# Listing the far tokens earlier, all row statistics between search rounds, normalising before the scatter

## The chip, the cores and the metric

The kernel runs on one core of a Trainium2 chip. The metric is device time in microseconds (us) of one launch: the median of three runs. The engines are PE (matrix products), DVE (VectorE, elementwise work), ACT (ScalarE, functions and scaled copies), POOL (GpSimd, here scatters, gathers and some additions) and SP (SyncE, here transfers only). Each works through its own queue in order and waits on semaphores for the others.

## The reference

Four images of 64 x 64 positions ("tokens", 4096 an image) with 256 channels. A deformable convolution comes first, then additive attention over each image's tokens, then a feed-forward layer on the higher-weighted half of the tokens only:

```python
# layer 0: x = x + conv(gn(x)); inside conv, every position, group and tap reads
samples = _bilinear_sample(img, sg)          # at learned offsets
out = (samples * m).sum(-1)                  # mask from a softmax over 9 taps
...
# layer 1
t = t + _L1_attn_ref(_ln_t(t), Wt, Wx, bh, Wa, ba)
t = t + _L1_ffn_ref(_ln_t(t), mask, wr, br, w1, b1, w2, b2)
...
def _L1_ffn_ref(x, attention_mask, wr, br, w1, b1, w2, b2):
    weights = (jnp.einsum('bsd,do->bso', x, wr) + br)[..., 0]
    _, idx = jax.lax.top_k(weights, k)       # k = half of 4096
    sel_idx = idx[:, :kk]                    # kk = k - 1
    sel = jnp.take_along_axis(x, sel_idx[:, :, None], axis=1)
    h = jax.nn.gelu(jnp.einsum('bkd,dh->bkh', sel, w1) + b1)
    y = jnp.einsum('bkh,hd->bkd', h, w2) + b2
    y = y * jnp.take_along_axis(weights, sel_idx, axis=1)[..., None]
    return jnp.zeros_like(x).at[batch_idx, sel_idx].set(y) + x
```

## The kernel before, in words

A first stage computes offsets and interpolation weights for all images, a second the convolution of image 0 (`sample_image(0, 6)`). Then a loop over the images n = 0 to 3 has two scopes each. In the first, three generators are stepped in turn by a string of letters (`turns`, L1418):

- "m" is `feed_forward(n - 1)` (L1244). It loads the attention's result as `v2` in 8 transfers (32 tiles of 128 tokens), takes 32 dot products `pr`/`tdot` with the router's weights (L1257, four steps of 8), forms the weights `wa`, and searches for the 2047th largest in 8 rounds of 4 bits each (`kth_largest`, L1201; a step per round). A round compares all weights with 15 candidates on DVE, sums over partitions with PE (`pcn`) and picks a digit. Then it turns two masks into positions (`positions`, L516, two matmuls and a prefix sum of 12 short operations), ends with the row numbers `rif`, and POOL scatters 32 tiles into sorted order in DRAM (`sort_d`, L1300); all that is the step after the last round. The next step writes the normalised tokens of all rows as `base` (ACT, L1312) to the output. Then it takes the sorted rows in chunks of 512: SP loads a chunk (`big<-sort`, L1332), which waits for all 32 scatters, ACT normalises it (L1340), PE transposes and multiplies.
- "o" is `attention_prep(n)` (L783). One step loads the tokens `v`; eight steps do `row_stats` of 4 tiles each (bn_stats and bn_aggr on DVE); one step makes the reciprocal deviation `lnr` (ACT, then DVE) and the shift `lnm`, and has ACT normalise the 32 tiles in place (L802). Then come three steps for each of 8 units: `units` (16 transposes `ptt` on PE, a copy `vT` to SBUF on DVE, a product `pq`), `products` (`pk`, `pf` on PE, `kf`, `qe` on ACT, a transfer `qf<-qe`, a minimum `least` on DVE), and `below_zero` (`mm` on DVE).
- "s" is `sample_image(n + 1)` (L668), empty for n = 3. Its first step is `list_tokens` (L534): some tokens' offsets are too far for the regular interpolation, and are listed. Flags `fl` become slots `sl` by `positions`, and 32 one-hot comparisons `oh` (DVE), each with a matmul into `pl` (PE), gather the listed tokens' numbers; `ls` and `uf` follow. The later steps are interpolations: a multiplication with interpolation weights `wb` (L697, one transfer of 512 KB each from SP, two buffers) and an addition (L705); `exact_rows` (L566 on) computes the listed tokens exactly, beginning with some 25 small DVE operations and a gather `rw` on POOL.

Operations of "m" and "o" on DVE are pinned: they keep their program order among themselves (L259). Those of `list_tokens` and `exact_rows` are not; the scheduler places them on DVE from where they stand in the program. For n = 0 another string is used, and m is empty. In the second scope of each image, attention runs (over 2000 us), with the rest of the "s" steps beside it. At the end, the feed-forward of image 3 runs alone.

The places in question are the three transitions between attentions: T1 (n = 1, lists image 2), T2 (n = 2, lists image 3) and T3 (n = 3, lists none). The lists of images 0 and 1 run in the convolution stage of image 0.

Of the kernel before, what the change touches and what calls it, by code (L numbers as in the profile page):

```python
# [9 lines left out]
F32 = mybir.dt.float32  # L10
I32 = mybir.dt.int32
AF = mybir.ActivationFunctionType
ALU = mybir.AluOpType
# [3 lines left out]
P = 128  # L17
NB, H, W, C = 4, 64, 64, 256
L = H * W
NT = L // P  # L20
# [25 lines left out]
def layers_kernel(ctx: ExitStack, tc: tile.TileContext, a, out: bass.AP):  # L46
    nc = tc.nc
# [162 lines left out]
    tok = cb.tile([P, NT, 2], F32, name="tok")  # L210
    slotr = cb.tile([P, P], F32, name="slotr")
# [22 lines left out]
    S = SimpleNamespace(bank=True, wants=False, gather=True, left=0, tables=[])  # L234

    def bank_taken():
        S.wants = not S.bank
        return S.wants

    @contextmanager  # L240
    def scope(*pools):

        with ExitStack() as st:
            for name, bufs, psum in pools:
                kw = {"space": PSUM} if psum else {}
                setattr(S, name, st.enter_context(tc.tile_pool(name=name, bufs=bufs, **kw)))
            yield
            for name, _, _ in pools:
                delattr(S, name)
# [267 lines left out]
    def positions(fl, vec):  # L517

        pp = S.ps_m.tile([P, 2, NT], F32, tag="pm", name="pp")
        nc.tensor.matmul(pp[:, 0, :], below, fl, start=True, stop=True)  # L520
        nc.tensor.matmul(pp[:, 1, :], ones, fl, start=True, stop=True)
        before = [S.two.tile([P, NT], F32, tag=f"bf{i}", name=f"bf{i}") for i in range(2)]
        vec.tensor_copy(before[0], pp[:, 1, :])
        for i in range(5):
            w = 1 << i
            vec.tensor_copy(before[1][:, :w], before[0][:, :w])
            vec.tensor_add(before[1][:, w:], before[0][:, w:], before[0][:, : NT - w])
            before.reverse()
        sl = before[1]
        vec.tensor_sub(sl, before[0], pp[:, 1, :])  # L530
        vec.tensor_add(sl, sl, pp[:, 0, :])
        return sl, before[0][:, NT - 1 :]

    def list_tokens(n):  # L534

        while bank_taken():
            yield  # L540
        fl = S.two.tile([P, NT], F32, tag="fl", name="fl")
        nc.vector.tensor_scalar(fl, omax[:, n, :], 1.0, None, ALU.is_gt)
        sl, total = positions(fl, nc.vector)
        nc.vector.tensor_copy(large[:, n : n + 1], total)

        nc.vector.tensor_scalar(sl, sl, 1.0, None, ALU.add)
        nc.vector.tensor_mul(sl, sl, fl)
        nc.vector.tensor_scalar(sl, sl, -1.0, None, ALU.add)
        pl = S.ps_m.tile([P, 2], F32, tag="pm", name="pl")
        for i in range(NT):  # L550
            oh = S.sb.tile([P, P], F32, tag="oh", name="oh")
            nc.vector.tensor_scalar(oh, slotr, sl[:, i : i + 1], None, ALU.is_equal)
            nc.tensor.matmul(pl, oh, tok[:, i, :], start=(i == 0), stop=(i == NT - 1))
        ls = S.two.tile([P, 2], F32, tag="ls", name="ls")
        nc.vector.tensor_copy(ls, pl)

        uf = S.smp.tile([P, 1], F32, tag="uf", name="uf")
        nc.vector.tensor_mul(uf, ls[:, 1:2], spare)
        nc.vector.tensor_sub(uf, spare, uf)
        nc.vector.tensor_add(uf, uf, ls[:, 0:1])  # L560
        return uf
# [106 lines left out]
    def sample_image(n, depth=1):  # L668
# [3 lines left out]

        S.left = STEPS
        uf = yield from list_tokens(n)
        yield
        exact = []
# [63 lines left out]
    def sample_any(n):  # L740

        num = nc.values_load(large[0:1, n : n + 1], min_val=0, max_val=L)
        with tc.If(num > P), scope(
            ("smp", 2, 0), ("two", 2, 0), ("sb", 2, 0), ("dn", 1, 0), ("ps_t", 1, 1), ("ps_m", 1, 1)
        ):
            cur = S.two.tile([P, 1], F32, tag="cur", name="cur")
            nc.vector.tensor_copy(cur, part)
            with tc.For_i(0, NT, 1):
                exact = []
                for _ in exact_rows(n, cur, exact):  # L750
                    pass
                put_rows(n, *exact[0])
                nc.vector.tensor_scalar(cur, cur, float(P), None, ALU.add)
# [649 lines left out]
    for n in range(NB):  # L1403
        with scope(("att", 1, 0), ("smp", 2, 0), ("dn", 1, 0)):
            v = S.att.tile([P, NT, C + 1], F32, name="v")
            kf = S.att.tile([P, 2, L], F32, name="kf")

            sampling = sample_image(n + 1) if n + 1 < NB else iter(())
            S.gather = False
            with scope(  # L1410
                ("one", 1, 0), ("two", 2, 0), ("sb", 2, 0), ("row", 2, 0), ("rp", 3, 0),
                ("ps_d", 2, 1), ("ps_n", 1, 1), ("ps_m", 3, 1),
            ):


                main = feed_forward(n - 1, pinned) if n else iter(())
                prep = attention_prep(n, v, kf, pinned)
                if n:  # L1418
                    turns = (
                        "mo" + "m" * 5 + "mo" * 6 + "m" + "ooo" + "s" + "oss" * 2 + "m" + "oss" * 7 + "m" + "oss" * 3  # L1420
                        + ("m" + "ossss" * 3 + "msss" * 4) * 4
                    )
                else:
                    turns = "o" * 10 + "s" + "os" * 24
                for turn in turns:
                    next({"m": main, "o": prep, "s": sampling}[turn], None)
                for rest in (main, prep):
                    for _ in rest:
                        pass
            S.gather = True  # L1430
            with scope(
                ("two", 2, 0), ("sb", 2, 0), ("rp", 6, 0), ("qp", 2, 0),
                ("ep", 2 * PVB + 1, 0), ("ap", 1, 0), ("ps_d", 2, 1), ("ps_n", 3, 1), ("ps_m", 1, 1),
            ):
                attention(n, v, kf, [sampling])
        attention_any(n)
        if n + 1 < NB:
            sample_any(n + 1)
# [39 lines left out]
```

## Time and profile before

| | us |
|---|---|
| median of 3 runs | 10557.95 |
| lowest and highest | 10553.36, 10569.91 |
| the profiled execution | 10563.61 |
| its span | 10561.9 |

The first transition, in the same execution (the last column is T2, where it was read):

| event | T1 | T2 |
|---|---|---|
| first DVE operation of the transition | 3615.64 | 5918.98 |
| weights `wa` begin | 3631.30 | 5932.86 |
| `rif`, the last thing before the scatter | 3679.97 | 5981.53 |
| first scatter on POOL | 3680.43 | 5982.00 |
| last scatter ends | 3720.7 | 6022.3 |
| list's result `ls` | 3730.93 | 6033.36 |
| third `vT` of the preparation | 3751.25 | 6053.69 |
| first operation on chunk 0 (`si`) | 3773.59 | 6075.91 |
| attention begins on PE | 3978.79 | 6280.00 |

How to read a line of a timeline: start in us, busy time in us, engine, source line, operation, written tile <- read tiles, shapes, count, and in brackets the idle time before it with what ended it. "issue" there means that the engine waited for nothing that the profile shows; "remote" names no instruction either; "DMA" with tiles is a transfer. A line that begins with a stretch A:B has its length and then busy time (and count) of each engine, the granted TensorE clock, the DMA engines' share of busy time and GB/s.

### The profile page before, as it was taken

The page shows a single profiled execution, that of the slowest core. Times are in us where ns is not written, and L with a number is a line of the kernel's source. Part 1 is how long each engine was busy: PE and PEld are TensorE (multiplying, and loading weights), DVE is VectorE, ACT ScalarE, POOL GpSimd, SP SyncE. Part 2 cuts the span into 40 slices and gives each one's busy share as a digit, 9 for nine tenths or more (in the row PEclk, how much of TensorE's full clock was granted, in tenths as well). Part 3 has the DMA queues.
Part 4 walks back from the last instruction along what each step waited for, and adds up shares of the span by engine and source line. Part 5 has one row for each costly group of instructions (what it writes and reads, how often), then busy time and mean ns, then how long its engine had stood idle before and what let it go on. Part 6 is the DMA issues. An engine that isn't in the chain of part 4 may idle for free. (4 is left out here: it accounts for less than half of the span.)

```text
span 10561.9 us, 115936 instructions
## 1 busy us (share of the span) xinstructions
PE 9008.4 (85%) x38460; PEld 4375.8 (41%) x38460; DVE 8547.2 (81%) x13406; ACT 7377.6 (70%) x8389; POOL 5265.2 (50%) x3059
## 2 busy tenths in 40 slices
PE   7882029999999678999999589999999699999995
PEld 4551014444444343444444344444444344444443
DVE  7776879898989778989899679899898357777772
ACT  4450018888888528888888438888888379999991
POOL 0004307676555326767655327676555155555552
PEclk8985569999999889999999789999999799999997
DMA  3336752222222252212111352222111300000002
GB/s 119 107 138 180 206 167 70 61 67 64 70 64 73 98 167 60 52 55 58 51 55 50 116 152 53 53 54 54 52 59 41 101 13 9 10 8 7 7 5 75
DMA packets 381330, 766.00 MB, mean 73 GB/s; under 512 B 49105, under 2 KB 212593, under 8 KB 380689
## 3 DMA queue, kind: packets, MB, share of 16 engines
q1 hardware_dynamic: 324432, 678.78, 20.3%
q0 software_dynamic: 30144, 45.87, 2.9%
q10 hardware_dynamic: 26112, 33.56, 0.9%
q8 instruction: 309, 5.06, 0.2%
q14 instruction: 333, 2.72, 0.1%
HBM read 580.88 MB, written 177.14 MB: 72 GB/s over the span
## 5 line engine op out<-in xcount | busy, mean ns | idle before, releaser
L909 DVE TENSOR_TENSOR r<-nn,r 128x512 f32<-128x512 f32 x6144 | 3943.0, 683 | 861.5 <-PE nn L904 805.9
L904 PE MATMUL nn<-qn,kf 32*128 32x512 f32 (+1 forms) x12288 | 4518.8, 640 | 132.7 <-DVE r L909 95.8
L994 POOL TENSOR_TENSOR r<-r 128x1024 f32<-128x1024 f32 x1024 | 2708.8, 2645 | 2645.4 <-DVE r L909 2625.3
L988 ACT ACTIVATE r<-d 128x1024 f32<-128x1024 f32 x3072 | 3117.2, 1015 | 1085.4 <-DVE r L998 699.9
L894 PE MATMUL d<-qf,kf 32*128 32x512 f32 (+1 forms) x12288 | 3338.1, 632 | 76.5 <-DMA qf<-qf 43.1
L990 ACT ACTIVATE r<-r 128x1024 f32<-128x1024 f32 x3072 | 3124.1, 1051 | 32.6
L904 PEld LDWEIGHTS nn<-qn,kf 32*128 32x128 f32 (+1 forms) x12288 | 1399.4, 185 | 1902.1 <-DVE r L909 1450.5
L932 PE MATMUL pv<-v,et 128*128 128x257 f32 x8192 | 2105.3, 400 | 15.0 <-DVE acv L956 15.0
L932 PEld LDWEIGHTS pv<-v,et 128*128 128x128 f32 x8192 | 1507.6, 194 | 975.5 <-issue 768.6
L894 PEld LDWEIGHTS d<-qf,kf 32*128 32x128 f32 (+1 forms) x12288 | 1018.0, 186 | 1340.3 <-issue 736.1
L996 POOL TENSOR_TENSOR r<-r 128x512 f32<-128x512 f32 x1024 | 1335.8, 1304 | 92.7 <-DVE r L909 17.1
L705 DVE TENSOR_TENSOR ac<-ac,prd 128x1024 f32<-128x1024 f32 x768 | 991.8, 1291 | 8.8
L697 DVE TENSOR_TENSOR prd<-xs,wb 128x1024 f32<-128x1024 f32 x768 | 977.7, 1273 | 15.2 <-DMA wb<-wt 12.0
L626 POOL DMA_INDIRECT ga<-tab,tii x576 | 718.3, 1247 | 207.3 <-issue 117.7
L916 ACT ACTIVATE et<-et,nshift 128x512 f32<-128x512 f32 x1024 | 723.8, 707 | 28.2 <-DVE et L1001 28.2
L998 DVE TENSOR_TENSOR r<-r 128x512 f32<-128x512 f32 x1024 | 723.6, 707 | 4.1 <-POOL r L994 3.7
L1001 DVE TENSOR_TENSOR et<-r 128x512 f32<-128x512 f32 x1024 | 698.1, 682 | 0.4
L115 ACT ACT_TABLE_LOAD x9 | 11.5, 1283 | 799.3 <-DVE mv L259 703.0
L721 PE MATMUL pmo<-outwp,ac 128*128 128x256 f32 x512 | 135.7, 416 | 469.1 <-DVE ac L705 431.2
L480 POOL MEMSET w<- 128x1600 f32 x16 | 22.9, 1432 | 675.0 <-PE ptw L497 352.3
L721 PEld LDWEIGHTS pmo<-outwp,ac 128*128 128x128 f32 x512 | 100.8, 205 | 521.4 <-DVE ac L705 304.5
L420 PE MATMUL pc<-xn,diag 128*128 128x512 f32 x576 | 262.2, 609 | 33.4 <-ACT xn L366 33.4
(344 smaller groups left out, 5282.7 us busy)
## 6 DMA issues: line engine op xcount, KB each, us to landing
wb<-wt SPq DMA_DIRECT2D x800, 512.0 KB
tab<-tb SPq DMA_DIRECT2D x128, 256.0 KB
v<-t SPq DMA_DIRECT2D x64, 512.0 KB
xs<-xp SPq DMA_DIRECT2D x32, 680.0 KB
xp<-xp SPq DMA_DIRECT2D x32, 544.0 KB
xt<-in_x_dram SPq DMA_DIRECT2D x32, 512.0 KB
xr<-in_x_dram SPq DMA_DIRECT2D x64, 256.0 KB
t<-xr SPq DMA_DIRECT2D x64, 256.0 KB
```

The lines of the kernel that those rows point to most:

```text
L697: keep(nc.vector.tensor_tensor(pr.rearrange("p (r w) -> p r w", w=W), src, wb.rearrange("p (r w) -> p r w", w=W), ALU.mult,))
L705: keep(nc.vector.tensor_add(ac[:, f, :], ac[:, f, :], pr))
L894: keep(nc.tensor.matmul(d[:, j, :], kf[g, blk, rows(kt)], qs[q][0][g, blk, :], start=True, stop=True))
L904: keep(nc.tensor.matmul(nn, kf[g, blk, rows(kt)], qs[q][1][g, blk, :], start=True, stop=True))
L909: keep(nc.vector.tensor_tensor(r[:, j, :], ns[j], r[:, j, :], ALU.mult))
L916: keep(nc.scalar.activation(ets[b], ets[b], AF.Exp, bias=nshift))
L932: keep(nc.tensor.matmul(pv, ets[b0 + i][:, rows(j)], v[:, k0 + i, :], start=(i == 0), stop=(i == PVB - 1)))
L988: keep(nc.scalar.activation(rs[b, p], ds.pop((b, p)), AF.Ln))
L990: keep(nc.scalar.activation(rs[b, p], rs[b, p], AF.Exp, scale=-1.0))
L994: keep(nc.gpsimd.tensor_tensor(rs[b, 1], rs[b, 1], rs[b, 2], ALU.add))
L996: keep(nc.gpsimd.tensor_tensor(rs[b, 1][:, 0], rs[b, 1][:, 0], rs[b, 3][:, 0], ALU.add))
L998: keep(nc.vector.tensor_add(rs[b, 1][:, 1], rs[b, 1][:, 1], rs[b, 3][:, 1]))
```

## The change

The string of turns for n > 0 is another, with the same number of steps of each kind in all. The first "s" step (the list) now comes right after the first "m" and "o" steps (after 8 of the 32 dot products and the issue of both token loads) instead of after the scatter. After the remaining dot products, each of the 8 search rounds is followed by one group of row statistics (before: 6 of the 8), and the step with `lnr`, `lnm` and the 32 normalisations on ACT comes before the step with positions and scatter instead of after it. Before, two groups of statistics, this step and the list came after the scatter in program order.

In `list_tokens`, two one-hots are made by one instruction: 16 comparisons of 128 x 2 x 128 elements with both operands broadcast, in place of 32 comparisons with a scalar per partition. Each feeds two matmuls.

```diff
         pl = S.ps_m.tile([P, 2], F32, tag="pm", name="pl")
         for i in range(NT):
-            oh = S.sb.tile([P, P], F32, tag="oh", name="oh")
-            nc.vector.tensor_scalar(oh, slotr, sl[:, i : i + 1], None, ALU.is_equal)
-            nc.tensor.matmul(pl, oh, tok[:, i, :], start=(i == 0), stop=(i == NT - 1))
+            if i % 2 == 0:
+                oh = S.sb.tile([P, 2, P], F32, tag="oh", name="oh")
+                nc.vector.tensor_tensor(
+                    oh, slotr.rearrange("p (o q) -> p o q", o=1).to_broadcast([P, 2, P]),
+                    sl[:, i : i + 2].rearrange("p (t o) -> p t o", o=1).to_broadcast([P, 2, P]), ALU.is_equal,
+                )
+            nc.tensor.matmul(pl, oh[:, i % 2], tok[:, i, :], start=(i == 0), stop=(i == NT - 1))
...
                     turns = (
-                        "mo" + "m" * 5 + "mo" * 6 + "m" + "ooo" + "s" + "oss" * 2 + "m" + "oss" * 7 + "m" + "oss" * 3
+                        "mos" + "m" * 3 + "mo" * 8 + "om" + "oss" * 2 + "m" + "oss" * 7 + "m" + "oss" * 3
                         + ("m" + "ossss" * 3 + "msss" * 4) * 4
                     )
```

In the order that the build gives each engine for T1 and T2, the list's positions stand between the first 8 dot products on DVE, and its 16 pairs before the other 24; the small operations of `exact_rows` stand in the first three search rounds, the gather `rw` stands ahead of the scatters on POOL, and `lnr` and `lnm` before the search's result `kres`. PE does 9 of unit 0's 16 transposes between the two `positions`. SP has five `wb` transfers ahead of `big<-sort` of chunk 0 (before: four) and one between those of chunks 0 and 1 (before: none). On ACT, four of the chunk's eight first normalisations stand before `qe` of the second unit and four after it; before, all eight stood before `kf` of the second unit. Lines of the changed kernel are four higher from L555 on.

## The prediction

> **What bounds the kernel now.** I read the page first, then a table by stretch around the change from image 0 to image 1 (the transition T1), then the timelines of VectorE, PE and SyncE there, and last the same place before image 3 (T3), where no far tokens are listed.
>
> ```profile
> span 10561.9 us, 115936 instructions
> PE 9008.4 (85%) x38460; PEld 4375.8 (41%) x38460; DVE 8547.2 (81%) x13406; ACT 7377.6 (70%) x8389; POOL 5265.2 (50%) x3059
> ...
> 3607.00:3632.00 25.00, 0.00 (x0) 0.00 (x0) 16.51 (x87) 1.76 (x3) 0.15 (x1) 0.54 0.82 270
> 3632.00:3680.00 48.00, 8.79 (x32) 7.65 (x32) 35.55 (x176) 17.33 (x32) 0.00 (x0) 0.50 0.66 220
> ...
> 3690.00:3731.00 41.00, 12.23 (x50) 10.05 (x50) 5.04 (x18) 14.16 (x28) 23.40 (x25) 0.50 0.23 82
> 3731.00:3784.00 53.00, 43.18 (x83) 16.72 (x84) 48.69 (x71) 11.21 (x15) 4.23 (x2) 0.67 0.55 161
> 3784.00:3964.00 180.00, 152.36 (x510) 94.36 (x508) 147.75 (x143) 52.77 (x63) 34.13 (x22) 0.94 0.58 187
> ```
>
> Most of the span is four attention stages of some 2300 us that the change leaves alone. The table's columns are length, busy time of PE, PE weight loads, DVE, ACT and POOL, granted clock, DMA share and GB/s. T1 is three things in a row. From 3616 to 3680 VectorE sets the pace (35.55 of 48 us in the search). From 3680 to 3721 POOL issues 32 scatters (one each 1.267 us: 40.3 us), and VectorE does only 5.04 of 41 us. From 3731 on VectorE is full again (48.69 of 53). What VectorE does in that gap:
>
> ```profile
> 3698.77 0.44 DVE L552 TENSOR_SCALAR oh<-slotr,bf 128x128 f32<-128x128 f32 x1 [4.62 <-remote]
> ...
> 3720.53 0.29 DVE L552 TENSOR_SCALAR oh<-slotr,bf 128x128 f32<-128x128 f32 x1 [7.38 <-remote]
> ...
> 3751.25 1.22 DVE L259 COPY vT<-ptt 128x1024 f32<-128x1024 f32 x1
> ...
> 3757.16 1.22 DVE L697 TENSOR_TENSOR prd<-xs,wb 128x1024 f32<-128x1024 f32 x1
> ```
>
> The list of far tokens crawls: one-hots wait 4.6 to 7.4 us for something the profile calls remote. Alone, a list takes 0.97 us for two one-hots and their matmuls, even beside loads at a DMA share of 0.70 (the window 852 to 872):
>
> ```profile
> 820.08 15.51 PE L553 MATMUL pl<-tok,oh 128*128 128x2 f32 x64 [3.17 <-DVE oh L552]
> ...
> 851.69 0.18 DVE L542 TENSOR_SCALAR fl<-omax 128x32 f32<-128x32 f32 x1 [15.90 <-DMA tab<-zm]
> ...
> 871.70 0.16 DVE L555 COPY ls<-pl 128x2 f32<-128x2 f32 x1 [0.68 <-PE pl L553]
> ```
>
> The natural hope is to free VectorE during the scatter. T3 shows what it then does: no list, and still
>
> ```profile
> 8283.38 0.18 DVE L259 CAST rif<-bf 128x32 int32<-128x32 f32 x1
> ...
> 8307.07 1.23 DVE L259 TENSOR_REDUCE least<-pk 128x1 f32<-128x1024 f32 x1 [8.54 <-ACT kf L828]
> 8314.10 0.75 DVE L259 TENSOR_SCALAR mm<-pq,bqk 128x512 f32<-128x512 f32 x1 [5.81 <-issue]
> 8328.83 1.23 DVE L259 COPY vT<-ptt 128x1024 f32<-128x1024 f32 x1 [13.98 <-remote]
> ```
>
> There the third vT comes 45.45 us after rif, 4.7 us after the last scatter left POOL (8324.1). The crawl goes with the scatter, not with the list.
>
> **The change, part by part.** Sums are made against the profiled execution, 10563.6 us (span 10561.9 and 1.7 around it). The median of the runs is 10557.95, 5.7 lower; I carry the difference over to it.
>
> *One-hots in pairs.* 32 tensor_scalar of 0.286 us become 16 tensor_tensor of 256 elements; the nearest row with two tensor inputs of that size (pr, 128x256) is 0.42 us. VectorE does 6.7 instead of 9.2 us, under PE, whose four matmuls took 0.97 us a pair with hand-overs and 0.86 later in T1 when fed without a gap. A list goes from 15.5 to 13.8 us. The list at 820 us is followed by a DMA wait of 15.9 us that hides it; the one at 851.69 ends just ahead of the first interpolation (872.4): -1.7 us, between -1.7 and 0 if PE still waits.
>
> The Trainium skill (VectorE: DVE Perf Modes, section "The perf-mode tier table") speaks against the pair: fp32 tensor_tensor runs at one element a cycle where tensor_scalar has two. By that alone a pair would cost 0.13 us more, an estimate of 2.1 us more a list; the rows give 0.42 against two times 0.286, so the fixed cost outweighs it.
>
> *The list moves ahead of the tokens' dot products (T1 and T2).* In the built order its positions stand between the first 8 dot products, and the 16 pairs ahead of the other 24. From fl to uf the list at 851.69 took 20.7 us. Less 1.7 for the pairs that is 19.0, the upper end; less the dot products' load waits in T1 (0.78, 0.55, 1.03) and the positions' PE wait of 1.16, which the two now fill for each other, it is 15.5, the lower end. I take 16.6, nearer the lower since both fillers are there. It isn't hidden by the loads: the 32 dot products already ran from 3617.67 to 3631.2 with 2.4 us of waiting.
>
> *All statistics between rounds.* A group of four rows is 2.11 us (rounds are 5.11 us apart with it, 3.0 without); two more groups: +4.2 us ahead of the scatter (T1, T2, T3).
>
> *Exact rows.* With the list early, its index and weight operations (3.9 us between 3740.74 and 3744.67) fall in the first search rounds. Each round leaves 0.70 us while PE sums: 2.1 in three rounds, so +1.8 (0 to 3.9). Their first one waits for the gather rw, now ahead of the 32 scatters on POOL, whose landing took 4.3 us at 874.9; about 3 us of search steps lie between (0 to 4): +1 (0 to 3). On POOL nothing else waits behind it then. Behind this wait stands the whole search, as VectorE keeps its order.
>
> *Reciprocal and shift of the normalisation.* They now stand before kres, behind ACT's lnr (0.32 us): ACT wait 0.4, then 0.35 and 0.19: +1.0. ACT's 32 normalisations (15.84 us) then run beside the positions, which hide them; without that cover they'd be where they are now, beside the scatter.
>
> *The tail.* Without the list woven in, kres to rif took 9.06 us in T3 (from 8274.32) against 9.85 in T1 (from 3670.12): -0.8.
>
> Sum to rif: 16.6 + 4.2 + 1.8 + 1 + 1.0 - 0.8 = +23.8. So rif moves from 3679.97 to 3703.8 in T1, from 5981.53 to 6005.3 in T2, and the scatter with it (its end is 40.7 us after rif). In T3 rif moves by 4.2 + 1.0 = +5.2.
>
> The Trainium skill (SBUF — State Buffer, section "SBUF: two separate sides") has VectorE's two-port operations lock GpSimd out while it writes descriptors, which would make the scatter faster without one-hots beside it: an estimate of 24 times 0.29, -7 us in T1 and T2. The row says no: 40.3 us with 24 one-hots, 40.25 in T3 without.
>
> *What the moved work gives back.* After the scatter VectorE takes up its list of work at a later item. Two rows bound where. Lower gain: T3's own crawl, third vT 45.45 us after rif: 3749.2 instead of 3751.25, -2.0 in T1; 6050.8 instead of 6053.69, -2.9 in T2. Upper gain: VectorE isn't held at all and does interpolations until the weights run out. wb has two buffers; the changed order on SyncE has five wb, then big<-sort, which waits for the scatter, with the sixth wb queued behind it:
>
> ```profile
> 3649.04 92.32 SPq L688 DMA_DIRECT2D wb<-wt  x4
> 3741.67 0.92 SPq L1332 DMA_DIRECT2D big<-sort  x2
> 3748.30 40.03 SPq L688 DMA_DIRECT2D wb<-wt  x11
> ```
>
> So the sixth multiplication can't start before the scatter's end (3744.5), 0.9 of issue and at most 5.3 of landing (3748.30 to the fifth at 3753.63): 3750.7 instead of 3757.16, -6.4 in T1, and likewise 6052.2 instead of 6059.60, -7.3 in T2. I take the lower gains, as T3 is the same preparation beside the same scatter; but ACT's queue there holds kf of the second unit behind the chunk's eight normalisations, and the changed order only qe behind four, so they may be exceeded.
>
> *T3.* The chunk's data are 5.2 us later; the preparation starts up to 4 us earlier against rif, since two groups (4.3 us) no longer follow it. +3, between -1.5 and +5.2.
>
> Total: -1.7 - 2.0 - 2.9 + 3 = -3.6: 10560.0 for the profiled execution, 10554.4 beside the median; I write 10554. From vT on, the same operations follow in the same order to the end, so nothing is late next but the FFN by as much as its chunk.
>
> **The rivals.**
> *A, faster:* the preparation isn't held beside the scatter. For it: T3's first 23.7 us after rif run freely, and the list isn't there now. Against: the 5.81 and 13.98 us above, in T3. It takes the upper gains (-6.4 - 7.3), T3's -1.5, the first list's -1.7, and, where the search too costs its lower ends (1.1 + 1.8 + 1 = 3.9 less, twice), comes to -24.7, or 10533. It decides where both hold.
> *B, slower:* hand-overs crawl beside the token loads as beside the scatter. For it: DMA is at 0.82 there, and T3's dot products show one stall of 2.86 us for no visible cause. Against: the list at 851.69 kept its 0.97 us at 0.70. At the crawl's pace (eight steps from the one-hot at 3688.88 to that at 3724.03: 4.4 us each) 2.4 pairs instead of 12 are done in the some 10.5 us from the first pair (about 3621.5) to 3632, where the loads of v2 have landed: 10.5 - 2.4 x 0.86 = +8.4 to rif. And beside the later scatter VectorE gets no further than the first least, resuming 3.3 us after it as in T1 now (3724.03 against 3720.7): 3756.2 instead of 3744.67 (+11.5), 6057.7 instead of 6047.11 (+10.6), T3 +5.2. Total +27.3: 10585. It decides from about 1.7 us a pair (5.2 us lost a list instead of 8.4: together +21).
> *C, no gain anywhere:* attention waits for its qf anyway (13.9 us at 3978), so T1 to T3 give 0 and the first list its -1.7: 10556, on the main case's side. Against: qf comes out of the preparation that moves.
>
> **How the numbers follow.** The forecast with C: 0.48, since T3's row is direct; A 0.20; B 0.32, more than A as everything is now later and has to be made up. About 0.2% (21 us) is what a measurement here can tell. The forecast's own range is 10541 (upper gains with the search terms as taken: -16.9) to 10571 (lower gains, T3 +5.2, the first list 0, and the search terms' upper ends, 2.4 + 2.1 + 2 = 6.5 more, twice: +13.3). The range reaches to both rivals with some 2 to 4 us of their own spread, 10531 to 10589. A gives faster 0.20, B slower 0.32.
>
> **What will show it.** List: its pairs at 0.86 to 1 us between 3620 and 3640. Search: rif near 3704. Crawl: third vT near 3749 with long remote waits before it (mine), or five interpolations done by 3745 (A). SyncE: big<-sort straight after the scatter. Wrong would be: pairs over 1.7 us, rif after 3710 (B), or anything in attention that changed its pace.

## The result, and the profile after

| | before | after |
|---|---|---|
| median of 15 runs each, us | 10560.94 | 10550.61 |
| lowest and highest | 10543.44, 10573.17 | 10531.18, 10568.60 |
| the profiled execution, its span | 10563.61, 10561.9 | 10547.94, 10546.2 |

The ratio is 0.9988, with a 95% interval of 0.9980 to 0.9996: 4 to 21 us faster, around the 0.2% that a measurement of this kernel can tell. The page's head after the change:

```profile
span 10546.2 us, 115935 instructions
...
PE 9022.3 (86%) x38460; PEld 4384.6 (42%) x38460; DVE 8536.6 (81%) x13342; ACT 7374.7 (70%) x8389; POOL 5276.0 (50%) x3059
```

VectorE has 64 instructions fewer (two transitions and two lists of the first stage, 16 each); the counts of the other engines are the same. What changed besides is the order. T1 in stretches (length; PE, weight loads, DVE, ACT, POOL; granted clock, DMA share, GB/s): list and dot products, search, scatter, the first chunk's start, the rest up to attention.

```profile
3610.00:3655.00 45.00, 15.93 (x72) 15.66 (x72) 27.32 (x143) 4.84 (x8) 1.16 (x2) 0.53 0.76 236
3655.00:3705.00 50.00, 10.40 (x41) 8.78 (x41) 39.16 (x181) 23.21 (x45) 0.00 (x0) 0.50 0.40 136
3705.00:3746.00 41.00, 28.00 (x44) 10.57 (x44) 18.10 (x17) 11.56 (x19) 31.05 (x32) 0.54 0.42 149
3746.00:3784.00 38.00, 23.69 (x39) 9.96 (x40) 26.24 (x25) 8.12 (x12) 4.26 (x2) 0.51 0.52 174
3784.00:3976.00 192.00, 153.35 (x512) 94.53 (x511) 148.73 (x147) 52.74 (x63) 38.58 (x24) 0.92 0.53 177
```

Beside the scatter VectorE now works 18.10 us. The 41 us from `rif` on in the kernel before (the 5.04 us that the prediction gives for the scatter belong to 3690 to 3731, which begins 10 us after `rif`):

```profile
3680.00:3721.00 41.00, 13.13 (x47) 10.91 (x47) 9.64 (x42) 17.44 (x34) 30.83 (x32) 0.50 0.28 101
```

So it is 18.10 against 9.64 us. The list has left that place. VectorE's timeline where the list now is:

```profile
3627.42 0.76 DVE L553 TENSOR_TENSOR oh<-slotr,bf 128x256 f32<-128x256 f32 x2
...
3640.04 0.42 DVE L553 TENSOR_TENSOR oh<-slotr,bf 128x256 f32<-128x256 f32 x1 [0.43 <-PE pl L557]
3641.75 0.16 DVE L559 COPY ls<-pl 128x2 f32<-128x2 f32 x1 [1.28 <-PE pl L557]
```

16 pairs take 14.33 us from the first one-hot to `ls`, against 50.5 us for 32 one-hots before (3680.40 to 3730.93). No wait in it is longer than 1.28 us, though the DMA share is 0.76. And VectorE from the end of the search:

```profile
3705.03 0.18 DVE L259 CAST rif<-bf 128x32 int32<-128x32 f32 x1
...
3725.51 1.23 DVE L259 COPY vT<-ptt 128x1024 f32<-128x1024 f32 x1 [1.90 <-remote]
...
3734.75 1.22 DVE L709 TENSOR_TENSOR ac<-ac,prd 128x1024 f32<-128x1024 f32 x1
3755.30 1.22 DVE L701 TENSOR_TENSOR prd<-xs,wb 128x1024 f32<-128x1024 f32 x1 [19.33 <-DMA wb<-wt]
...
3771.60 2.31 DVE L259 TENSOR_SCALAR si<-big 128x4 int32<-128x4 f32 x1
```

Three copies `vT` and five interpolations are done within 31 us of `rif`. Then VectorE stands still for 19.33 us with all that it could do behind the sixth multiplication, whose weights `wb` are late. SyncE's timeline says why (the last scatter starts at 3745.96):

```profile
3663.30 56.75 SPq L692 DMA_DIRECT2D wb<-wt  x5
3750.05 0.71 SPq L1336 DMA_DIRECT2D big<-sort  x1
3750.78 0.00 SPq L692 DMA_DIRECT2D wb<-wt  x1
```

`big<-sort` waits for the scatter at the head of SyncE's queue, and the sixth `wb` goes out directly after it. ACT stands behind the same chunk, with its normalisations in front of `qe` and the next `kf`:

```profile
3752.36 2.07 ACT L1344 ACTIVATE big<-big 128x256 f32<-128x256 f32 x4 [18.78 <-DMA big<-sort]
```

In T3, which has no list, VectorE shows:

```profile
8307.99 0.75 DVE L259 TENSOR_SCALAR mm<-pq,bqk 128x512 f32<-128x512 f32 x1 [9.03 <-remote]
8325.52 1.22 DVE L259 COPY vT<-ptt 128x1024 f32<-128x1024 f32 x1 [16.78 <-remote]
...
8332.89 0.16 DVE L259 TENSOR_SCALAR si<-big 128x4 int32<-128x4 f32 x1
```

The `vT` at 8325.52 is 45.60 us after `rif` (8279.92), as the third was before (45.45). But it is the fourth: the third was at 8293.95. The stall stayed, and one copy more, with what hangs on it, was done ahead of it.

I measure a transition from the last statistics of one attention to the first product `d` of the next one on PE. Three profiles of the kernel before and two of the changed one, taken along with the experiments (r1, r2, r3 below), give:

| us | T1 | T2 | T3 |
|---|---|---|---|
| before | 368.90 | 367.04 | 291.90 |
| before, r1 | 373.83 | 369.27 | 290.84 |
| before, r3 | 371.26 | 370.73 | 291.12 |
| after | 365.80 | 358.49 | 288.70 |
| after, r2 | 363.78 | 366.99 | 288.62 |
| difference of the means | -6.5 | -6.3 | -2.6 |

The parts that the change doesn't touch vary as well. Attention 1 took 1934.58 us in the first profile of the changed kernel and 1943.25 us in r2, with the same instructions, and T2 of the changed kernel differs by 8.5 us between its two profiles. So single profiles give a transition to about 5 us at best. (An attention takes 1816 to 2024 us in these five; the "some 2300 us" of the prediction is an attention with its transition.)

### The profile page after: what moved, and what is told of

Its sections match the earlier page's. It is cut to its first block, busy times and chain, and to the rows that moved or that the text cites. A ratio compares the mean times of both kernels' runs of the same rounds, so it can differ in the third digit from the quotient of the medians.

```text
span 10546.2 us, 115935 instructions
## 1 busy us (share of the span) xinstructions
PE 9022.3 (86%) x38460; PEld 4384.6 (42%) x38460; DVE 8536.6 (81%) x13342; ACT 7374.7 (70%) x8389; POOL 5276.0 (50%) x3059
```

## Experiments

The times of before given here are the medians of the runs beside each set. The kernels e1 to e4 share 30 of them (10561.06 us). Each takes one part of the change alone or away. Diffs are against the changed kernel where nothing else is said.

**e1: the new order, with one-hots one by one.**

```diff
-            if i % 2 == 0:
-                oh = S.sb.tile([P, 2, P], F32, tag="oh", name="oh")
-                nc.vector.tensor_tensor(oh, ...
-                ...
+            oh = S.sb.tile([P, P], F32, tag="oh", name="oh")
+            nc.vector.tensor_scalar(oh, slotr, sl[:, i : i + 1], None, ALU.is_equal)
-            nc.tensor.matmul(pl, oh[:, i % 2], ...
+            nc.tensor.matmul(pl, oh, ...
```

> The new string of turns with the old one-hots, one by one. Lengths of a transition are from the last row statistics of an attention to the first product of the next: before 368.9 (T1), 367.0 (T2), 291.9 (T3), changed 365.8, 358.5, 288.7. Theory V (what VectorE does beside the scatter pays; the list costs its length): a list takes 15.9 us from the first one-hot to ls instead of 14.3, rif and the scatter come 1.6 us later, so T1 and T2 are 1 to 2 us longer than in the changed kernel, T3 the same; the time is within 0.1% of the changed kernel, about 10553. Theory P (the pairs make the gain, by half the hand-overs while tokens load): one-hots wait over 1.5 us each beside the loads, T1 and T2 are 5 to 8 us longer, the time is about 10563.

Measured: 10583.92 us, 1.0019 (1.0009 to 1.0028). The transitions took 368.42, 363.51 and 288.46 us, 7.4 us less in sum than before; the list took 15.9 us in both. The loss isn't there but in the attentions 1 and 2: 1941.96 and 1946.96 us against 1934.17 and 1933.59. The whole attention 1 of the changed kernel and of e1, each in one row:

```profile
3976.00:5911.00 1935.00, 1870.72 (x8294) 863.30 (x8294) 1734.45 (x2614) 1645.15 (x1792) 1235.70 (x686) 0.98 0.19 53
```

```profile
3976.00:5918.00 1942.00, 1875.69 (x8294) 866.40 (x8294) 1737.43 (x2614) 1647.49 (x1792) 1239.90 (x685) 0.98 0.19 52
```

The counts are equal but for one instruction of POOL at the edge, and PE is busy 5 of the 7 us longer, with the same 8294 matmuls: most of the loss isn't a new wait. Neither theory's time came (10553, 10563). What holds from the run is the list's pace, and that VectorE again waits for the sixth `wb`:

```profile
DVE prd L697 <- DMA wb<-wt: 29.2, 2, 28.5
```

(Waits by engine and line: total, times, longest.) What the pairs are worth by themselves isn't shown by it.

**e2: the pairs alone.** The kernel before, with only the new `list_tokens`:

```diff
-                        "mos" + "m" * 3 + "mo" * 8 + "om" + "oss" * 2 + "m" + "oss" * 7 + "m" + "oss" * 3
+                        "mo" + "m" * 5 + "mo" * 6 + "m" + "ooo" + "s" + "oss" * 2 + "m" + "oss" * 7 + "m" + "oss" * 3
```

> The kernel before, with paired one-hots; the order of turns is the old one, so the list stands beside the scatter. Theory H (each hand-over from PE to VectorE is slow beside the scatter, some 4.4 us): about 7 pairs are done before the crawl, 8 crawl, ls comes near 3724 instead of 3731, T1 and T2 are 6 to 7 us shorter than before (about 361) without any change of order. Theory S (the list ends when the scatter ends, whatever is left): ls near 3727 to 3731, T1 and T2 0 to 4 us shorter. T3 as before (292) by both. Time: H 10546, S 10555.

Measured: 10553.96 us, 0.9994 (0.9984 to 1.0004), no difference that can be told. `ls` came 45.7 us after `rif` in both transitions, against 51.0 and 51.8 before. Half as many hand-overs save only 5 of 51 us, because each that is left waits longer:

```profile
DVE ls L559 <- remote: 17.8, 1, 17.8
DVE oh L553 <- remote: 15.7, 3, 6.6
```

T1 was 362.89 us, T2 365.99; T3, which the edit doesn't reach, was 295.55, 4 us longer than in the profiles of before. So neither a fixed price for each hand-over nor a list that ends with the scatter's last piece describes it; the measured value lies between.

**e3: everything but the early list.** Statistics between all rounds, normalisation ahead of the scatter, pairs, but the list after the scatter again:

```diff
-                        "mos" + "m" * 3 + "mo" * 8 + "om" + "oss" * 2 + ...
+                        "mo" + "m" * 3 + "mo" * 8 + "om" + "s" + "oss" * 2 + ...
```

> The changed kernel with the list after the scatter step again (paired one-hots kept): all statistics and the normalisation stay early. Theory V: T3 as in the changed kernel (289); rif 5 us later than before (3685, relative to the start of T1), the list crawls beside the scatter, and holds PE and VectorE, so vT comes after it; T1 and T2 are 0 to 5 us longer than with pairs alone, near 366 to 370. Theory N (the early normalisation is what pays, the list is neutral): T1 and T2 are as in the changed kernel or shorter (365 and 358 or less).

Measured: 10540.09 us, 0.9981 (0.9972 to 0.9991). T1 was 356.23, T2 362.18, T3 287.36: in T1 and T2 together 17.5 us less than in the first profile before, and 5.9 less than in the first after. The list took 24.5 and 25.8 us beside the scatter, half of what it took before. VectorE's row beside the scatter, and a wait of the list:

```profile
3690.00:3731.00 41.00, 26.86 (x78) 18.23 (x79) 14.74 (x45) 8.74 (x17) 30.21 (x31) 0.51 0.33 120
```

```profile
DVE ls L559 <- remote: 6.6, 1, 6.6
```

T1 came as theory N expected (365 or less), T2 between N's 358 and V's 366. Against e2, which differs from e3 only in the place of statistics and normalisation, the three transitions are 6.7, 3.8 and 8.2 us shorter, each between single profiles. Listing while the tokens load isn't what pays. It moves 16.6 us of VectorE work ahead of the scatter, and VectorE later waits 19.33 us for `wb`.

**e4: the early list and the pairs, but statistics and normalisation at their old place.**

```diff
-                        "mos" + "m" * 3 + "mo" * 8 + "om" + "oss" * 2 + ...
+                        "mos" + "m" * 5 + "mo" * 6 + "m" + "ooo" + "oss" * 2 + ...
```

> The changed kernel with the statistics and the normalisation where they were (six of eight groups between rounds, two and the normalisation after the scatter step), the list early and paired. Theory V: rif 5 us earlier than in the changed kernel; five interpolations still fit beside the scatter, and the sixth follows its end, so T1 and T2 are up to 5 us shorter than changed (361 and 353), T3 as before (292); time about 10543. Theory N (the early normalisation pays): the preparation is caught in the crawl as in T3 of before, least of the first unit comes after the scatter, T1 and T2 are as before or longer (367 to 372); time 10560 or more.

Measured: 10582.49 us, 1.0023 (1.0012 to 1.0033). T1 368.28, T2 366.16, T3 290.28: in sum 3 us less than before, with about 19 us more in the attentions 1 and 2 (1942.24 and 1944.75). Third `vT` 3746.38, with remote waits ahead of it again. So the list's move alone gains nothing in the transitions, which agrees with e3. The median, 21 us above before, can't be put down to the transitions, since the 19 us lie in stages with unchanged work.

The next four are a second session. The kernel before took 10538.81 us beside them (21 runs), 22 us less than beside the first set, and neither of the two lists that stand wholly beside the scatter there (e6, e7) crawled. The changed kernel wasn't run beside these four, so what is set against it below comes from the first set.

**e5: `big<-sort` issued by POOL**, to take it out of the way of the sixth `wb`:

```diff
-            get = nc.sync.dma_start(
+            get = nc.gpsimd.dma_start(
```

> The changed kernel with the loads of the sorted chunks issued on POOL's queue, behind the scatters, instead of SyncE's. In the changed kernel VectorE waits 19.3 us in T1 for the sixth wb, which stands behind big<-sort. Theory W (that wait limits what the change gives): interpolations 6 to 8 run beside the scatter, the wait goes, T1 and T2 are 4 to 6 us shorter than changed (361 and 353), T3 the same (289), time about 10541. Theory D (chunk data and the feed-forward bound the stage anyway): the 19 us wait moves to another releaser, T1 and T2 stay within 2 us of 365.8 and 358.5, time 10548 to 10555.

Measured: 10567.20 us, 1.0031 (1.0018 to 1.0045). The sixth multiplication came at 3724.03 instead of 3755.30, the `wb` wait was gone, and this stood in its place:

```profile
DVE least L259 <- ACT kf L832: 26.9, 3, 24.3
```

ACT has the chunk's eight normalisations ahead of this `kf` in its queue (four in front of the `qe` before it), and the first waits for the chunk:

```profile
3749.74 2.07 ACT L1344 ACTIVATE big<-big 128x256 f32<-128x256 f32 x4 [28.12 <-DMA big<-sort]
```

`si` came 160.9 us after the end of attention 0, against 158.6 after the change: all interpolations that were done earlier gained nothing for the chunk. The scatter, which the chunk waits for, took 43.5 us from `rif` to the start of its last instruction against 40.9. T1 and T2 were 367.98 and 371.96, no shorter than in the two profiles of the changed kernel. The wait has moved from SyncE's queue to ACT's, as theory D expected, but T2 and the time lie above D's figures (within 2 us of 358.5, 10548 to 10555).

**e6: the kernel before, with every scatter done twice** (the second time into a spare table, so that POOL scatters some 85 us):

```diff
+            ins = nc.gpsimd.indirect_dma_start(
+                out=sort2_d[n], out_offset=bass.IndirectOffsetOnAxis(ap=ri[:, i : i + 1], axis=0),
+                in_=v[:, i, :], in_offset=None,
+            )
```

> The kernel before, with every scatter issued twice, the second into a spare table: POOL is busy some 81 us instead of 40. Theory C (PE's hand-overs are slow as long as scatters run): the list crawls on, its last result ls comes 85 to 95 us after rif instead of 51, and one-hots keep waiting 3 to 8 us each until then. Theory F (the crawl is a fixed number of slow steps, or the cold PE): ls comes about 51 us after rif as before, while the scatter still runs. By both the chunk's data come some 40 us later four times, time about 10700 to 10720.

Measured: 10659.79 us (one run). With twice the scatter beside it, and with the one-by-one list of the kernel before, the list took 18.7 us. PE's timeline there:

```profile
3684.93 7.34 PE L554 MATMUL pl<-tok,oh 128*128 128x2 f32 x28 [0.19 <-DVE oh L553]
```

28 matmuls in 7.34 us, without a stall. Neither theory came: C expected `ls` 85 to 95 us after `rif`, F 51, and it came after 19.1; the time is also below their 10700. The scatter is not enough to make the hand-overs slow.

**e7: e3 with e5's edit.**

> The version with the list late (all statistics and the normalisation early, paired one-hots), and the chunk loads on POOL's queue. There the interpolations begin only after the list, near the scatter's end, so by theory W and by theory D SyncE's queue does not hold them: T1 and T2 within 3 us of that version's 356 and 362, time 10536 to 10546. A gain of more than 5 us in T1 or T2 would mean that SyncE held more than the wb transfers.

Measured: 10530.65 us, 0.9996 (0.9986 to 1.0006). T1 352.63, T2 354.01. The list stands right beside the scatter and takes 14.3 us, as it does ahead of the scatter in the changed kernel:

```profile
3676.56 0.82 DVE L553 TENSOR_TENSOR oh<-slotr,bf 128x256 f32<-128x256 f32 x2
...
3678.94 0.42 DVE L553 TENSOR_TENSOR oh<-slotr,bf 128x256 f32<-128x256 f32 x1 [0.43 <-PE pl L557]
```

T2 is 8.2 us shorter than in e3, more than the 5 us that the expectation set as the mark. But the list is 10 us shorter than e3's as well, so what of this comes from SyncE's queue isn't shown. Beside the kernel before of its own session no gain can be told.

**e8: the list woven into the search.** It is cut into ten steps, one after each search round, so that it fills the time in which VectorE waits for PE's sums; e5's edit is kept:

```diff
+        if n > 1:
+            yield
         pl = S.ps_m.tile([P, 2], F32, tag="pm", name="pl")
         for i in range(NT):
...
             nc.tensor.matmul(pl, oh[:, i % 2], tok[:, i, :], start=(i == 0), stop=(i == NT - 1))
+            if i % 4 == 3 and n > 1:
+                yield
...
-                        "mos" + "m" * 3 + "mo" * 8 + "om" + "oss" * 2 + ...
+                        "mo" + "m" * 3 + "s" + "mos" * 8 + "om" + "s" + "oss" * 2 + ...
```

> Paired one-hots, all statistics and normalisation early, chunk loads on POOL, and the list cut into ten steps: positions before the search, two pairs of one-hots a round (placed by the scheduler between the first rounds), the end after the scatter step. Theory V: the pairs' 6.7 us and the positions' 3 to 4 us of VectorE partly fill the 0.7 us holes of the rounds, so the list costs 6 to 9 us of the path instead of 16.6; rif 6 to 10 us earlier than changed, less up to 7 us for unit 0's first operations, which the scheduler puts ahead of rif; T1 and T2 353 to 360, time 10525 to 10540. Theory G (what attention's granted clock does hides such gains): T1 and T2 as said, but time within 10 us of the changed kernel's 10551.

Measured: 10520.19 us, 0.9985 (0.9975 to 0.9995). T1 342.27, T2 346.62, the shortest of all and below the 353 to 360 expected; T3 was 294.71. Against e7 of the same session, in which the list stands in one piece after `rif`, T1 and T2 are 10.4 and 7.4 us shorter.

**r1 and r2: the kernel before and the changed one again, unedited.** The second set's pace had to be told from that of the first.

> The kernel before once more, profiled again. In the runs so far PE's signals were slow beside the scatter in the first two sets (kernel before: the list takes 50.5 us from its first one-hot) and quick in the third (a list beside the scatter 14.3 and 18.7 us), in which the kernel before was also 22 us faster. Theory K (the slow hand-overs are a state of the chip used, not of the kernel): where the list takes under 25 us, T1 and T2 are 8 to 20 us shorter than 368.9 and 367.0 and the time is near 10539; where it takes over 40 us, the time is near 10561. Theory O (they come from the order of the kernel before): the list takes 45 to 52 us again, whatever the time. The ratio to itself should be within 0.1% of 1.

> The changed kernel once more, on the same chip as the run before it. Theory K: if the list of the kernel before takes under 25 us there, the changed kernel has nothing to win by moving it and pays 16.6 us ahead of the scatter: T1 and T2 not shorter than those of the kernel before by more than 3 us, ratio 0.999 to 1.003. If it takes over 40 us, T1 and T2 are 3 to 9 us shorter and the ratio is 0.998 to 1.000 as at first. Theory O: the ratio is 0.998 to 1.000 in any case.

Measured, on the chip of the second set but later: the kernel before 10565.03 us in the runs beside them and 10562.78 in r1; the changed one 10562.16, 0.9994 (0.9984 to 1.0003). The crawl was back, 51.6 us for the list in r1:

```profile
DVE oh L552 <- remote: 26.0, 5, 8.1
```

In r2 VectorE again waited for the sixth `wb` (multiplication at 3758.93). T1 and T2 of the two differ by 10.0 and 2.3 us. For a list over 40 us theories K and O expected nearly the same, so this doesn't decide between them.

**r3 and r4: the kernel before a third time, and e8's once more**, on another chip.

> The kernel before, a look at its list on this chip today. Theory K (slow hand-overs beside the scatter are a state of the chip): either the list takes over 40 us and the time is 10550 to 10575, or it takes under 25 us, T1 and T2 are 355 to 362 and the time is 10525 to 10550. Theory O (they belong to the kernel before): over 40 us whatever the time.

> The woven version again (list in ten steps, statistics and normalisation early, pairs, chunk loads on POOL). In the set in which hand-overs were quick it took 0.9985 of the kernel before, 10520. Theory K: if the list of the kernel before takes over 40 us here, that kernel loses its crawl on top, and the woven version, which has little to hand over beside the scatter, keeps its T1 and T2 of 342 and 347 within 6 us: ratio 0.996 to 0.9975, about 10525 to 10535. If under 25 us, the ratio is 0.998 to 0.9995 again. Theory G (the clock in attention decides): ratio 0.998 to 1.0 in either state.

Measured: before 10560.24 (9 runs), r3 10558.61 (one run), r4 10521.44, 0.9964 (0.9950 to 0.9977). The crawl was there, 51.6 us for the list of r3:

```profile
DVE oh L552 <- remote: 30.6, 6, 8.1
```

T1 and T2 of r4 were 345.50 and 348.84. PE and SyncE in r4:

```profile
3649.59 1.01 PE L559 MATMUL pl<-tok,oh 128*128 128x2 f32 x4 [1.66 <-DVE oh L555]
3652.38 0.61 PE L1215 MATMUL pcn<-kpart,ones 128*128 128x15 f32 x2 [1.77 <-DVE kpart L259]
```

```profile
3649.39 149.45 SPq L696 DMA_DIRECT2D wb<-wt  x22
```

List and search alternate on PE, and SyncE issues 22 `wb` without standing behind a chunk. The list is done (3659.12) 28.7 us before `rif`. So the time of this version doesn't depend on the crawl: it was 10520 us in the session without it and 10521 us in one with it, on two chips, while the kernel before took 10539 and 10560. It beats the kernel before, by 38 us (0.36%, interval 0.23 to 0.50%) in the last session; the changed kernel, which was never run beside it, stood at 0.9988 and 0.9994 of the kernel before. K's ratio (0.996 to 0.9975) came, and G's 0.998 lies just outside the interval. What it still waits for is ACT, as e5: `kf`, 28.7 us.

The kernels of e8 and r4 are the same, and T3 shows both states. VectorE in e8 (`rif` 8251.65), then PE and VectorE in r4 (`rif` 8250.94):

```profile
8272.44 1.23 DVE L259 COPY vT<-ptt 128x1024 f32<-128x1024 f32 x1 [0.27 <-PE ptt L788]
```

```profile
8276.53 2.44 PE L841 MATMUL pf<-mm,sel 64*128 64x512 f32 x4
8288.00 0.75 DVE L259 TENSOR_SCALAR mm<-pq,bqk 128x512 f32<-128x512 f32 x1 [12.79 <-issue]
8296.45 1.23 DVE L259 COPY vT<-ptt 128x1024 f32<-128x1024 f32 x1 [7.70 <-remote]
```

The fourth `vT` comes 20.8 us after `rif` in e8 and 45.5 us in r4; there PE's products had ended some 9 us before VectorE and ACT (`qe`, 8287.99) went on. So the program doesn't decide whether the hand-overs are slow. In T3 the slow ones cost nothing: it took 290.30 us in r4 and 294.71 in e8, where `kf` waits 27 us for the chunk instead.

## Why the prediction was right, and where it was wrong

The predicted time, 10554, is 3.4 us above the measured median. The sum behind it was -3.6 us; the three transitions changed by -15.4 us between the means of the table, and the medians by -10.3 us in the first set and -2.9 us beside r2 (interval -17 to +3 us). That 10554 lies so near is in part luck: the kernel before stood at 10557.95 when the forecast was made and at 10560.94 beside the result. The end is thus better than the step that carried the forecast.

*To rif: +23.8 predicted, +21.9 measured in T1 and +20.7 in T2* (from the attention's end). The list was exact: `wa` begins 16.6 us later in T1 and 15.7 in T2. From `wa` to `kres` the changed kernel took 45.11 against 38.82 us, so +6.3 where 8.0 stood. T3, which has no exact rows, gives the same +6.3 (45.03 against 38.75). So the exact rows and their wait for `rw`, +2.8 in the sum, cost nothing: the search's waits for PE hide them. Statistics, `lnr` and `lnm` cost 6.3 instead of 5.2. The tail was -0.94 against -0.8.

*"The crawl goes with the scatter, not with the list"; third vT "by T3's row", 45.45 us after rif.* This is the step that failed, with the term that it gave: lower gains of -2.0 and -2.9 us. The third `vT` came 20.5 us after `rif` in T1, 20.0 in T2 and 14.0 in T3, and in r2 17 to 18 us in all three. T3's row was true but its position was misread. I had noted that T3's first 23.7 us run freely (8.54 of them were a wait for ACT's `kf`); in T3 before, two groups of statistics, `lnr`, `lnm` and the wait for the first normalised tiles took the first 9 us, and the change moves them ahead of `rif`. With them gone, three copies `vT` fit in ahead of the stall, and the crawl (27 us in T3's two waits of 9.03 and 16.78, with the `mm` between) hits the fourth. I had counted this as "up to 4 us earlier", a shift of the whole, where the first `vT` came 8.9 us earlier against `rif` (0.09 against 8.97), instead of asking which instruction then stands at the stall. And the sentence itself is wrong as a rule: beside the scatter the list took 18.7 us in e6 and 14.3 in e7, against 15.9 and 14.3 ahead of it (e1, the changed kernel).

*The upper gain.* It came true, as the prediction's limit and rival A's mechanism: VectorE does interpolations until the sixth `wb`, which stands behind `big<-sort`. It was to start at 3750.7 and did at 3755.30, as `rif` was 1.2 us later (attention 0 had ended 3.1 us later in this profile), the scatter took 1.1 us longer, and `big<-sort` went out about 3 us after it; the landing took 4.5 us instead of 5.3. `si` came 5.1 us earlier against the attention's end in T1 and 8.4 in T2, and over all profiles T1 and T2 gained 6.5 and 6.3 us, for which -6.4 and -7.3 were worked out; with single profiles 5 us apart, so close a match is partly chance. I took the lower gains because T3 seemed the same preparation beside the same scatter.

*T3: +3 predicted, -2.6 measured*, by the same misreading: its `rif` and scatter are 6.2 us later, and one `vT` more is done ahead of the stall.

*The first list: -1.7 predicted, not shown.* The first interpolation came 4.1 us earlier in the first profile, but r1, the kernel before, has it at 867.59 too, ahead of the changed kernel's 868.28. The pair's 0.86 us held.

*The rivals.* B (hand-overs crawl beside the token loads) is excluded: every pair took 0.86 us at a DMA share of 0.76, and `rif` came before its point of decision, 3710. A's mechanism decided T1 and T2, but not its sum: its lower search terms didn't all come, and an end of -24.7 us wasn't reached. C (no gain in any transition) is spoken against by the means of all three, though T2 in r2 (366.99) comes close to it.

*Where the expected gain went.* VectorE was freed of 50 us of crawling list. 16.6 us of that were paid ahead of the scatter instead, 6.3 us by the search, and 19.3 us in the wait for `wb`. e3 against e2 shows which part pays beside a crawl: statistics and normalisation ahead of the scatter, 18.7 us less in the three transitions and 14 us in the median with the list at the same place. In the session without the crawl, e7, with the same order and the chunk loads on POOL, shows no gain that can be told. The list pays where its price is hidden, in the search's gaps (e8 against e7).

Open: what makes the hand-overs slow. It isn't the scatter alone (e6, e7), nor the program (T3 of e8 and r4), and the chip used doesn't settle it either: the second set without it and r1 with it ran on the same one, though with different kernels. The kernel before was not profiled in the quick session; that its 22 us come from there is concluded from e6's list (18.7 instead of 51 us) and from the median of the kernel before, not shown.

## What to carry to other kernels

When work is removed ahead of a stall, ask which instruction will stand at the stall then, and don't carry over the time of the one that stood there before. A queue in order (here SyncE's, then ACT's) that holds one instruction waiting for a late event holds all behind it: find the next such queue before the first is cleared, as e5 only moved the wait. Freed time pays where the moved work falls into waits that another engine causes anyway; moved to a place where its own engine sets the pace, it costs its full length.

## What the hardware showed unexpectedly

- PE's signals reach VectorE late beside the scatter in some sessions (waits of 2 to 17.8 us, called remote) and not in others: 51 us against 18.7 us for the same 32 one-hots and matmuls (r1 and e6, on the same chip, e6 with a doubled scatter), and in one and the same kernel a fourth `vT` 45.5 or 20.8 us after `rif` (r4, e8).
- Attentions 1 and 2, with the same number of instructions on PE, VectorE, ACT and POOL in all 14 profiles, took between 1926.8 and 1947.0 us. In the six longest (over 1941 us) the mean granted clock over the attention, worked out from the trace, was 0.977 to 0.980, in the six shortest (under 1932.1) 0.983 to 0.985. Over the 15 runs of the changed kernel, a mean granted clock lower by 0.001 goes with about 9 us more (0.915: 10563 us, 0.918: 10537 us). e1 and e4, slower than before by 20 us with shorter transitions, had mean clocks of 0.9148 and 0.9158 against 0.9171 of before. Whether the order of work in the transitions sets this clock wasn't tried.
- The scatter is held up by VectorE's interpolations. From `rif` to the start of its last instruction it took 39.8 us in T1 before, 39.7 or 39.8 in T3 of before, after, r1 to r4, but in T1 40.9 after, 43.7 in r2 and 44.5 in r4, where more tensor_tensor work runs beside it. POOL and VectorE in T1 of r2:

```profile
3717.16 0.96 POOL L1304 DMA_INDIRECT sort<-v,rif  x1 [0.30 <-issue]
...
3724.91 1.95 POOL L1304 DMA_INDIRECT sort<-v,rif  x1 [0.30 <-issue]
```

```profile
3717.21 1.22 DVE L709 TENSOR_TENSOR ac<-ac,prd 128x1024 f32<-128x1024 f32 x1
...
3724.81 1.22 DVE L709 TENSOR_TENSOR ac<-ac,prd 128x1024 f32<-128x1024 f32 x1
```

  The scatter that begins 0.05 us before an addition takes its usual 0.96 us; the one that begins 0.10 us after an addition takes 1.95, as if it waited for the addition's end (3726.03). Five such overlaps in T1 of r2 (0.5 to 1.0 us each) give the 4 us. In the 14 profiles all 83 scatters of over 1.1 us (of 1920) begin inside a tensor_tensor of two SBUF tensors; the copies `vT`, which read PSUM, lengthen none. The Trainium skill (SBUF — State Buffer, section "SBUF: two separate sides") calls the port pair that VectorE and GpSimd share an exclusive lock, which the one that starts first has for its whole instruction, and names VectorE operations with two SBUF inputs among those that take it against a GpSimd operation that reads SBUF. The lines agree where the addition comes first. Where the scatter comes first they show no wait: the addition 0.05 us behind it takes its usual 1.22 us. The prediction had found no such price with one-hots beside the scatter (22 of them, not 24), which held for these tensor_scalar operations, and had not asked it for the interpolations that took their place. The paired one-hots are tensor_tensor too: beside them five scatters of e2 were lengthened, to 1.26 us at most.
